# A four-layer modulated convolution: the third weight combination with 19 products in borrowed banks, and another order of the iterations from quad 4 on

## The chip, the core and the metric

The kernel runs on one core of one Trainium2 chip. The time is the device time of one execution in microseconds (us). Three executions of the kernel before gave 480.82, 481.82 and 482.02 us; their median, 481.82 us, is the time before.

## The reference

The input `x` holds 128 samples of 64 channels and 1024 positions, the style `cond_512` a vector of 128 for each sample. Four layers follow one another, and their result is added to `x`:

```python
TYPES = ('same', 'upsample', 'same', 'downsample')
s = style @ mw.T + mb
weight = SCALE * w * s[:, None, :, None]
demod = lax.rsqrt(jnp.sum(weight * weight, axis=(2, 3)) + EPS)
weight = weight * demod[:, :, None, None]
```

Each layer is a convolution with three taps of 64 by 64 channels, with the sample's own weights, and a bias. The second layer doubles the length and blurs, the fourth blurs and halves it. Nothing nonlinear lies between the layers, so for each sample the four of them are one convolution with nine taps, but for a few positions at both ends.

## The kernel before, in words

**The work.** Four samples make a *quad*; there are 32 quads, q = 0 to 31. The 128 partitions hold 64 channels of two samples, and two column blocks the other two, so each product appears as four matmuls of 64 rows by 64 columns (upper and lower half of the rows, upper and lower half of the columns). Everything is in 32-bit floats, and the profile shows each of these matmuls as two, eight for a product.

For each quad the nine taps are made first, in three *weight combinations* on TensorE (PE), each followed by ScalarE (ACT) copies that scale the result out of the PSUM accumulators:

- `stage1` combines the weights of layers 4 and 3 into the tile `S`. From quad 4 on it is split: `stage1_a` (three products, five blocks of 64 columns) and `stage1_b` (two products, two blocks). VectorE (DVE) forms two further blocks from the accumulators (L443), and GpSimd (POOL) adds one block into another (L446, called the S addition below).
- `stage2` applies the blur and layer 2 (tile `E`) and gives seven blocks `R`. In its plain form it has 9 products with 23 blocks (L533). Where it is *shared*, `share_sums` adds blocks of `S` on DVE (L462), `share` computes three products into unused columns of the accumulator `psA` of another quad (L467), `share_copy` lets ACT copy them into `psR` (L490), and `stage2_rest` adds the other 14 products. Quads 7 to 30 are shared.
- `stage3` (L574) combines `R` with layer 1 (`w0s`) to the nine taps `Wf`. It has 9 products: six in part 0 with 14 blocks and three in part 1 with 7 blocks, 21 blocks of 64 columns in all. ACT scales them into `Wf` (L361). 

**The convolution** of a quad is done in Winograd's way: positions come in threes, and five products `conv0` to `conv4` with 340 columns (each with three tap groups, 24 matmuls in the profile, all on L685) take the place of nine. Its inputs are sums of shifted rows of `x`: `in3`, `in_g01`, `in_g2` and `in04` on DVE, `in1` (L658) and `in2` (L663) on POOL from quad 4 on. `in1` and `in2` need the sums `G` that `in_g01` and `in_g2` leave. Its weights are sums of taps, `combine_a` and `combine_b` on DVE (tile `H`), and `residual` adds the identity. conv3 opens the accumulator `psA`, ACT copies it out (`copy_m3`), conv1 adds to it and DVE's `sum1` reads it; then conv2 adds to it, and DVE's `sum2` writes two results: the accumulator `Y` (the bank that conv4 adds to) and the tile `y`. conv0 adds to `psA` at the end. ACT scales the three results `psA`, `Y`, `y` into `o` (`output`, L753), and SP stores them. Loads of `x` are also on SP's queue.

**The order** is written out by hand: the loop at L1207 issues for each q the instructions of several quads, and each engine executes its own in that order. In iteration q the quad q ends (conv4, conv0, outputs), n = q+1 has conv3, conv1 and conv2, c = q+2 has stage2 and stage3 and its inputs, and s = q+4 (from q = 3 on) has stage1. The weight combinations use two PSUM banks, `ps_w`, one after another; `psA` has two buffers of two banks, `Y` two banks.

**One-time work** lies in the dictionary `EXTRA`, (q, place): the normalisations (`var_newton`), scale tables on POOL (`table_C` writes `tC`, the scale of `R`, for all quads from 8 on), and the outputs at both ends of the samples, which are computed apart: `SLOTS` names the iterations (9, 12, 14, 19) with an additional group of end products on PE in `Y`, and `setup_x`, `setup0`, `setup1`, `setup3`, `rest0` to `rest3`, `rest1_bias` and `blur_side` are their DVE steps. `ends3` in iteration 28 is the last end product, `rest3` and `rest3_bias` its DVE steps.

Of the kernel before, what the change touches and what calls it, by code (L numbers as in the profile page):

```python
# [55 lines left out]
K = 3  # L56
# [7 lines left out]
def kernel(  # L64
# [26 lines left out]
    r_pool = ctx.enter_context(tc.tile_pool(name="r_pool", bufs=4))  # L91
# [58 lines left out]
    Z = const.tile([P, 512], F32, name="Z")  # L150
# [272 lines left out]
    def stage1_a(q):  # L423

        ps = unit(ps_w, f"psS{q}")
# [25 lines left out]
    Ed = const.tile([P, 6, C], F32, name="Ed")  # L451
# [69 lines left out]
    def stage2(q, pool=None, engs=(nc_a, nc_a), between=None):  # L521
# [21 lines left out]
        rt = []  # L543
        for r in range(2):
            t = r_pool.tile([P, 7, C], F32, tag="R", name=f"R{q}_{r}")
            scaled_copy(
                engs[r], t.rearrange("c t o -> c (t o)"), ps[r][:, : 7 * C], tC[:, q, r : r + 1]
            )
            rt.append(t)
        chain[q] = rt  # L550
        return ps

    def stage3(q, part, pool=None, engs=(nc_a, nc_a)):

        rt = chain[q]
        ps = unit(pool or ps_w, f"psW{q}_{part}")
        if part == 0:
            Wq[q] = (
                wf_pool.tile([P, 2, K, K, C], F32, tag="Wf", name=f"Wf{q}"),
                wf_pool.tile([P, 3, 2, K, C], F32, tag="H", name=f"H{q}"),  # L560
            )
        W = Wq[q][0]
        kinds = ((0, 1), (2,))[part]
        n = 0
        for i, kind in enumerate(kinds):
            for k in range(K):
                gs = [g for g in range(K) if 0 <= K * g + kind - k < 7]
                lo, m = gs[0], len(gs)
                first = K * lo + kind - k
                n += 1  # L570
                for r, rows in enumerate(HALF):
                    for c, cols in enumerate(HALF):
                        at = (K * i + lo) * C
                        nc.tensor.matmul(  # L574
                            ps[r][cols, at : at + m * C],
                            w0s[kind][rows, k, :],
                            rt[c][rows, first : first + K * (m - 1) + 1 : K, :],
                            start=(n == 1),
                            stop=(n == K * len(kinds)),
                            skip_group_check=True,  # L580
                        )
        for r in range(2):
            dst = W[:, r, kinds[0] : kinds[-1] + 1].rearrange("c t g o -> c (t g o)")
            scaled_copy(engs[r], dst, ps[r][:, : len(kinds) * K * C], t0[:, q, r : r + 1])
        return ps

    def residual(q):

        W = Wq[q][0]
        for r in range(2):  # L590
            v = W[:, r, 1, 1, :]
# [5 lines left out]
    def taps(q):  # L597
        W, H_ = Wq[q]
        return *(W[:, :, i] for i in range(K)), *(H_[:, i] for i in range(3))
# [74 lines left out]
    def product(q, m, ps, groups=range(K)):  # L674
# [3 lines left out]
        for g in groups:  # L678
            for s, rows in enumerate(HALF):
                for c, cols in enumerate(HALF):  # L680
                    if m in (0, 4):
                        w = W[rows, c, m // 2, g, :]
                    else:
                        w = H_[rows, m - 1, c, g, :]
# [24 lines left out]

    def conv3(q, pool=None):  # L710
        A[q] = unit(pool, f"psA{q}") if pool else ps_conv.tile([P, 2, 512], F32, tag="u", name=f"psA{q}")
# [448 lines left out]
    def layers(i, j):  # L1160
# [4 lines left out]
        (1, 1): lambda: small_rest(1),  # L1165
# [26 lines left out]
        (28, 1): rest3,  # L1192
        (28, 2): rest3_bias,
# [5 lines left out]
    AHEAD = 3  # L1199

    def sharing(q):
        return AHEAD < q < NQ - 4
# [4 lines left out]
    for q in range(NQ):  # L1207
# [4 lines left out]
        if n == NQ:  # L1212
            for i, queue in enumerate((nc.sync, nc_a)):
                output(q, 1, i, nc_v)
                store(q, i, slice(1, 2), queue)
            conv4(q)
            for i, (eng, queue) in enumerate(zip(BOTH, (nc.sync, nc_a))):
                output(q, 2, i, eng)
                store(q, i, slice(2, K), queue)
            conv0(q, *range(K))  # L1220
            for i, (eng, queue) in enumerate(zip(BOTH, (nc_a, nc.sync))):
                output(q, 0, i, eng)
                store(q, i, slice(0, 1), queue)
            break
        if c < NQ:
            stage2(c)
        if n < NQ - 1:
            sum2(q)
        if n < NQ - 1:
            if q == 0:  # L1230
                in_g01(n)
            if q == 1:
                in_g2(n)
                load(n + NX)
            combine_a(n)
            combine_b(n)
            if q == 0:
                in_g2(n)
                load(n + NX)

        if n == NQ - 1:

            conv3(n)
            copy_m3(n)
            conv4(q, 0, 1)
            for i in range(2):
                output(q, 1, i)
            conv1(n)
            sum1(n)
            conv4(q, 2)  # L1250
            for i in range(2):
                output(q, 2, i)
                store(q, i, slice(1, K))
            in04(n, PAIR[0])
            in04(n, PAIR[1])
            conv0(q, 0)
            conv2(n)
            conv0(q, 1, 2)
            sum2(n)
            for i in range(2):  # L1260
                output(q, 0, i)
                store(q, i, slice(0, 1))
            continue

# [13 lines left out]
        if late(q):  # L1278
            for i in range(2):
                store(q, i, slice(2, K))  # L1280
            if late(q - 1):
                for i in range(3):
                    load(c + 1, slice(i, i + 1))
        if c < NQ:
            stage3(c, 0)
        conv3(n)
        copy_m3(n)
        if sharing(q) and not sharing(q - 1):
            share_sums(c + 1)
# [9 lines left out]
        if c < NQ:  # L1299
            stage3(c, 1)  # L1300
        if q in SLOTS:
            slot(*SLOTS[q], Y_banks)
        if s < NQ:
            conv0(q, 0)
# [7 lines left out]
        elif s < NQ:  # L1312
            stage1_a(s)
        elif q == NQ - 4:
            slot(ends3, 3, unit(ps_w, "psE"), 3)
        conv1(n, 1, 2)
        for i in range(2):
            output(q, 1, i)
            if late(q):
                store(q, i, slice(1, 2))  # L1320
# [6 lines left out]
        if n == NQ - 2:  # L1327
            combine_a(n + 1)
            combine_b(n + 1, (0,))
# [4 lines left out]
        conv0(q, *((1,) if s < NQ else (0, 1)))  # L1334
        if twice:
            stage1_a(s)
        elif s < NQ:
            stage1_b(s)
        if sharing(q + 1) and not twice:
            share_sums(s)  # L1340
        if sharing(q):
            share(c + 1, banks(q))
        conv0(q, 2)
        if sharing(q):
            share_copy(c + 1)
# [10 lines left out]
        if q and c < NQ - 1:  # L1356
# [3 lines left out]
        if s + 1 < NQ:  # L1360
            scale3(s + 1)
# [3 lines left out]
        if n == NQ - 2:  # L1365
            sum2(n, (0,))
            combine_b(n + 1, (1,))
            in1(n + 1, nc_v)
            sum2(n, (1,))
            combine_b(n + 1, (2,))  # L1370
            in2(n + 1, nc_v)
        for i in range(2):
            store(q, i, slice(0, 1 if late(q) else K))

# [77 lines left out]
```

## Time and profile before

| what | value |
|---|---|
| median of three executions | 481.82 us |
| the profiled execution, its own time | 482.28 us |
| its span, first to last instruction | 480.4 us |
| PE, busy | 98% of the span |
| DVE, busy | 83% |
| ACT, busy | 63% |
| POOL, busy | 29% |
| mean granted TensorE clock | 0.997 of full speed |

The span is what the views count from: a start of 203.24 us is 203.24 us after the first instruction. PE stands for TensorE's matmuls and PEld for its weight loads. In a group of instructions, "out<-in" names the tiles with their numbers left out, and "x24" how often the instruction is there. The chain of work that ended last is followed back from the last instruction, at each step to what released it. A matmul's own duration contains time in which others run beside it; where matmuls follow one another in the chain, the length of the piece is what they cost.

### The profile page before, as it was taken

Reading aid. Unit: us, or ns where it says so; the run is one execution under the profiler, and the core shown is the slowest. Engines: PE = TensorE matmul, PEld = TensorE weight load, DVE = VectorE, ACT = ScalarE, POOL = GpSimd, SP = SyncE. Lnnn points to the kernel's source line nnn. Section 1 sums busy time; section 2 is a strip of 40 time slices with the busy share of each in tenths; the row PEclk is TensorE's granted clock in tenths of the full one; section 3 lists DMA queues with packets and bytes.
Section 4 is the critical chain, followed back from the end, with each engine's and each line's share of the span. In section 5 each row is a group of like instructions: output and inputs, shape, how many; then the busy total and the mean of one; then the engine's idle time right before and its main releaser. Section 6 shows DMA issues by size and latency. Waiting matters only on the chain.

```text
span 480.4 us, 25778 instructions
## 1 busy us (share of the span) xinstructions
PE 472.2 (98%) x11592; PEld 369.2 (77%) x11592; DVE 399.0 (83%) x660; ACT 303.8 (63%) x620; POOL 138.9 (29%) x171
## 2 busy tenths in 40 slices
PE   8999999999999999999999999999999999999995
PEld 7977787888788777878777798767777887877762
DVE  4899998799898888878868898758988887777984
ACT  5466666666667666766666666667666666665442
POOL 2533032635413333302333212333112333322100
PEclk9999999999999999999999999999999999999998
DMA  7116364245555346544445545345544445554314
GB/s 243 53 63 194 118 195 191 92 149 172 164 159 149 115 138 180 163 136 140 141 137 178 150 150 145 125 148 161 165 142 129 151 150 180 169 157 151 106 60 175
DMA packets 50494, 70.65 MB, mean 147 GB/s; under 512 B 5648, under 2 KB 47312, under 8 KB 50384
## 3 DMA queue, kind: packets, MB, share of 16 engines
q1 hardware_dynamic: 49792, 68.32, 44.7%
q8 instruction: 91, 1.49, 1.3%
q10 hardware_dynamic: 592, 0.69, 0.4%
q14 instruction: 19, 0.16, 0.1%
HBM read 35.36 MB, written 33.62 MB: 144 GB/s over the span
## 4 chain that ended last, share of the span: by engine, by line
PE 97%; DVE 2%; issue 0%; ACT 0%; ACTq 0%; DVEq 0%
PE psA L685 45%; PE psW L574 15%; PE Y L685 11%; PE psR L467 10%; PE psS L390 6%; PE psR L533 4%; PE psA L467 2%; PE Y L921 2%; PE Y L337 1%; PE Y L181 1%; DVE Oe L1011 0%; PE psM L205 0%; DVE o L755 0%; DVE y L595 0%; PE psE L921 0%
## 5 line engine op out<-in xcount | busy, mean ns | idle before, releaser
L685 PE MATMUL psA<-T,H 64*64 64x340 f32 x2304 | 193.3, 446 | 1.2 <-DVE y L595 0.9
L685 PEld LDWEIGHTS psA<-T,H 64*64 64x64 f32 x2304 | 100.2, 133 | 46.6 <-issue 3.3
L446 POOL TENSOR_TENSOR S<-S 128x128 f32<-128x128 f32 x28 | 15.0, 536 | 268.7 <-ACT S L361 261.5
L595 DVE SCALAR_TENSOR_TENSOR G<-X 128x684 f32<-128x684 f32 (+1 forms) x65 | 76.2, 1207 | 0.0
L685 PE MATMUL psA<-T,Wf 64*64 64x340 f32 x768 | 74.8, 446 | 0.0
L361 ACT ACTIVATE R<-psR,tC 128x448 f32<-128x448 f32 x63 | 36.5, 630 | 43.4 <-PE psR L467 26.8
L361 ACT ACTIVATE Wf<-psW,t 128x384 f32<-128x384 f32 (+1 forms) x126 | 56.3, 497 | 11.1 <-PE psW L574 10.8
L685 PE MATMUL Y<-T,Wf 64*64 64x340 f32 x768 | 62.9, 447 | 0.2 <-issue 0.2
L574 PE MATMUL psW<-R,w0s 64*64 64x128 f32 (+1 forms) x1536 | 63.1, 287 | 0.0
L574 PEld LDWEIGHTS psW<-R,w0s 64*64 64x64 f32 x1536 | 53.2, 133 | 5.9
L595 DVE SCALAR_TENSOR_TENSOR Y<-m,psA 128x680 f32<-128x680 f32 x32 | 27.8, 870 | 33.3 <-PE psA L685 33.3
L663 POOL TENSOR_TENSOR T<-G 128x684 f32<-128x684 f32 x28 | 50.9, 1817 | 0.0
L467 PE MATMUL psR<-S,E 64*64 64x64 f32 (+1 forms) x1536 | 50.6, 237 | 0.2 <-issue 0.2
L672 DVE TENSOR_TENSOR T<-G 128x1368 f32<-128x1368 f32 (+1 forms) x33 | 50.6, 1536 | 0.0
L658 POOL TENSOR_TENSOR T<-G 128x684 f32<-128x684 f32 x28 | 46.5, 1660 | 13.1 <-DVE G L595 13.1
L753 ACT ACTIVATE o<-Y,tb,td 128x340 f32<-128x340 f32 x63 | 36.6, 630 | 19.3 <-PE Y L685 16.7
L467 PEld LDWEIGHTS psR<-S,E 64*64 64x64 f32 x1536 | 43.2, 134 | 5.1 <-issue 0.3
L595 DVE SCALAR_TENSOR_TENSOR y<-psA,m 128x680 f32<-128x680 f32 x32 | 27.7, 865 | 23.1 <-PE psA L685 20.6
L390 PEld LDWEIGHTS psS<-wd,w2n 64*64 64x64 f32 x1120 | 38.3, 133 | 9.5
L685 PEld LDWEIGHTS Y<-T,Wf 64*64 64x64 f32 x768 | 32.9, 133 | 13.9 <-issue 1.1
L753 ACT ACTIVATE o<-psA,tb,td 128x340 f32<-128x340 f32 x63 | 37.0, 644 | 8.0 <-PE psA L685 8.0
L361 ACT ACTIVATE S<-psS,tBn 128x256 f32<-128x256 f32 x56 | 23.5, 470 | 28.2 <-PE psS L390 28.2
(153 smaller groups left out, 703.6 us busy)
## 6 DMA issues: line engine op xcount, KB each, us to landing
out<-o SPq DMA_DIRECT2D x167, 170.0 KB, 2.7
X<-in_x SPq DMA_DIRECT2D x150, 172.0 KB, 3.5
X<-in_x SPq DMA_DIRECT2D x14, 516.0 KB, 4.9
out<-o SPq DMA_DIRECT2D x6, 510.0 KB, 5.6
out<-o SPq DMA_DIRECT2D x2, 340.0 KB, 2.7
Xe<-in_x_ends SPq DMA_DIRECT2D x1, 512.0 KB, 6.5
out<-o ACTq DMA_DIRECT2D x3, 170.0 KB, 3.1
par<-in_params SPq DMA_DIRECT2D x2, 192.0 KB, 3.3
```

What stands on the lines that cost most here:

```text
L361: nc_a.activation(dst, src, AF.Copy, scale=f)
L390: nc.tensor.matmul(ps[r][cols, at * C : (at + n) * C], weight[rows], wd[c if r == 0 else 1 - c][rows, taps], start=first, stop=last, skip_ ...
L446: nc_g.tensor_add(t[:, :, 2], t[:, :, 2], t[:, :, 0])
L467: nc.tensor.matmul(dst[r][cols], weight[rows], st[c if r == 0 else 1 - c][rows, slots, :], start=False, stop=last, skip_group_check=True,)
L533: nc.tensor.matmul(ps[r][cols, lo * C : (lo + m) * C], E[rows, e + 2, :], src[rows, a, :], start=(n == 0), stop=(n == 8), skip_group_check ...
L574: nc.tensor.matmul(ps[r][cols, at : at + m * C], w0s[kind][rows, k, :], rt[c][rows, first : first + K * (m - 1) + 1 : K, :], start=(n == 1 ...
L595: nc_v.scalar_tensor_tensor(out, x, f, y, op0=ALU.mult, op1=op)
L658: eng.tensor_add(t[:, :, 0, :NJ], plane(g, 2), plane(g, 1))
L663: eng.tensor_sub(t[:, :, 1, :NJ], plane(g, 2), plane(g, 1))
L672: nc_v.tensor_sub(t[:, pairs, :, :NJ], both(a, PL), both(b, 1))
L685: nc.tensor.matmul(ps[s][cols, :NB], w, Ts[q, tag][rows, c, i, g : g + NB], start=(g == 0 and m == 3), stop=(g == K - 1), skip_group_check ...
L753: nc_a.activation(dst, src, AF.Identity, bias=add, scale=d3)
```

## The change

1. `stage3` becomes two parts for quads 6 to 30. `stage3_b` opens the accumulator `psA` of quad n, before conv3 of quad n opens it anew, and computes seven products with 12 blocks. Two of its seven result blocks are shares: ACT copies them (times 1 and times 1/3, four copies of 128x128) into `ps_w`, and `stage3_a` adds four products with 7 blocks there. Together 19 blocks in 11 products, where there were 21 in 9. Three new operands come with it: `Wd` (two differences of weights, on POOL in iteration 1), and two further blocks of `R`, which DVE adds for each quad (`r_sums`, 128x256, both inputs in `R`).
2. `R` is one tile of 2x9 blocks with two buffers instead of one of 7 blocks for each half with four; `Wf` has its taps in the order of their making; `Z` is smaller, and `Ed` lies in a tile that is no longer needed.
3. The loop is split. Iterations 0 to 3 keep the order before (`early_turn`). Iterations 4 to 28 have a new one (`turn_of`, 4 with some exceptions as the *entry*), in which conv2 of a quad moves behind the next iteration's stage2. Iterations 29 to 31 are written out. The extras of an iteration, which stood at three places in it, all come at its end. Sharing begins at iteration 5, so quads 8 to 30 are shared. `rest3` takes the place of `in_g01` in iteration 28, and `rest3_bias` moves to iteration 29.

```diff
-    r_pool = ctx.enter_context(tc.tile_pool(name="r_pool", bufs=4))
+    r_pool = ctx.enter_context(tc.tile_pool(name="r_pool", bufs=2))
...
+    def r_sums(q):
+        t = chain[q]
+        nc_v.tensor_add(t[:, :, 7:9], t[:, :, 2:6:3], t[:, :, 3:7:3])
...
+    def stage3_b(q, ps):
+        new_w(q)
+        t = chain[q]
+        plan = (
+            (slice(0, 3), w0s[2][:, 2, :], slice(0, 7, 3)),
+            (slice(0, 2), w0s[2][:, 1, :], slice(1, 5, 3)),
+            (slice(0, 2), w0s[2][:, 0, :], slice(2, 6, 3)),
+            (slice(3, 4), w0s[0][:, 0, :], slice(0, 1)),
+            (slice(4, 5), w0s[1][:, 0, :], slice(1, 2)),
+            (slice(4, 5), w0s[1][:, 1, :], slice(0, 1)),
+            (slice(5, 7), w0s[0][:, 1, :], slice(7, 9)),
+        )
+        for i, (at, weight, slots) in enumerate(plan):
+            same_row(blocks(ps, at), weight, t, slots, i == 0, i == len(plan) - 1)
+        pw = shared_w[q] = unit(ps_w, f"psW{q}")
+        src = blocks(ps, slice(5, 7))
+        for i, f in enumerate((1.0, 1.0 / 3.0)):
+            for dst, v in zip(blocks(pw, slice(i, i + 3, 2)), src):
+                scaled_copy(nc_a, dst, v, f)
+        stage3_out(q, ps, 0, 5)
+
+    def stage3_a(q):
+        t, pw = chain[q], shared_w.pop(q)
+        plan = (
+            (slice(0, 3, 2), Wd[:, 0], slice(3, 7, 3)),
+            (slice(0, 3, 2), w0s[0][:, 2, :], slice(1, 5, 3)),
+            (slice(1, 4, 2), Wd[:, 1], slice(2, 6, 3)),
+            (slice(1, 2), w0s[1][:, 0, :], slice(4, 5)),
+        )
+        for i, (at, weight, slots) in enumerate(plan):
+            same_row(blocks(pw, at), weight, t, slots, last=i == len(plan) - 1)
+        stage3_out(q, pw, 5, 4)
...
-        (28, 1): rest3,
-        (28, 2): rest3_bias,
+        (29, 0): rest3_bias,
...
     def sharing(q):
-        return AHEAD < q < NQ - 4
+        return FIRST < q < NQ - 4
...
+    def turn_of(q):
+        n, c, s = q + 1, q + 2, q + 4
+        entry = q == FIRST
+        stage2(c)
+        r_sums(c)
+        if not entry:
+            conv2(q)
+        sum2(q)
+        if entry:
+            conv4(q)
+        stage3_b(c, open_a(n))
+        combine_a(n)
+        if entry:
+            conv0(q, 0, 1)
+        else:
+            conv4(q)
+        stage3_a(c)
+        combine_b(n)
+        conv3(n)
+        if entry:
+            copy_m3(n)
+        outputs(q, 2)
+        for i in range(3):
+            load(c + 1, slice(i, i + 1))
+        if s < NQ:
+            stage1_a(s)
+        else:
+            slot(ends3, 3, unit(ps_w, "psE"), 3)
+        if not entry:
+            copy_m3(n)
+        in04(n)
+        in3(c)
+        if q in SMALL:
+            l, bs = SMALL[q]
+            nc_v.memset(high(bs.stop - bs.start), 0.0)
+        in_g2(c)
+        conv0(q, *((2,) if entry else range(K)))
+        if entry:
+            conv1(n, 0, 1)
+        outputs(q, 1)
+        if s < NQ:
+            stage1_b(s)
+            in_g01(c)
+        else:
+            rest3()
+        if sharing(q):
+            share(c + 1, banks(q))
+            share_copy(c + 1)
+        outputs(q, 0)
+        if q in SLOTS:
+            slot(*SLOTS[q], Y_banks)
+        if q in SMALL:
+            small(q)
+        conv1(n, *((2,) if entry else range(K)))
+        sum1(n)
+        if s == NQ:
+            in_g01(c)
+        if sharing(q + 1):
+            share_sums(s)
+        in1(c, nc_g)
+        in2(c, nc_g)
+        for i in range(3):
+            extra(q, i)
+        if s + 1 < NQ:
+            scale3(s + 1)
+
+    for q in range(FIRST):
+        early_turn(q)
+    for q in range(FIRST, NQ - 3):
+        turn_of(q)
+
+    q, n, c = NQ - 3, NQ - 2, NQ - 1
+    stage2(c)
+    conv2(q)
+    stage3(c, 0)
+    sum2(q, (0,))
+    combine_a(n)
+    sum2(q, (1,))
+    conv4(q)
+    combine_b(n)
+    conv3(n)
+    outputs(q, 2)
+    copy_m3(n)
+    extra(q, 0)
+    in04(n)
+    in3(c)
+    in_g01(c)
+    stage3(c, 1)
+    conv0(q, 0)
+    conv1(n)
+    outputs(q, 1)
+    in_g2(c)
+    sum1(n)
+    combine_a(c)
+    combine_b(c, (0,))
+    conv0(q, 1, 2)
+    outputs(q, 0)
+    conv2(n)
...
```

More of the change, by code (lines that the diff above doesn't have):

```diff
@@ L1211 @@
             nc.sync.dma_start(Xe, x_ends)
[L1212 to L1263, printed above, removed]
+        stage2(c)
+        sum2(q)
+        if q == 0:
+            in_g01(n)
+        if q == 1:
+            in_g2(n)
+            load(n + NX)
+        combine_a(n)
+        combine_b(n)
+        if q == 0:
+            in_g2(n)
+            load(n + NX)
         conv4(q)
@@ L1355 @@
             load(c + NX)
-        if q and c < NQ - 1:
+        if q:
             in1(c, nc_g)
@@ new lines @@
+    conv0(q, 1, 2)
+    outputs(q, 0)
+    conv2(n)
+    sum2(n, (0,))
+    combine_b(c, (1,))
+    in1(c, nc_v)
+    sum2(n, (1,))
+    combine_b(c, (2,))
+    in2(c, nc_v)
+    q, n = NQ - 2, NQ - 1
+    conv3(n)
+    copy_m3(n)
+    conv4(q, 0, 1)
+    for i in range(2):
+        output(q, 1, i)
+    conv1(n)
+    sum1(n)
+    conv4(q, 2)
+    for i in range(2):
+        output(q, 2, i)
+        store(q, i, slice(1, K))
+    in04(n, PAIR[0])
+    in04(n, PAIR[1])
+    conv0(q, 0)
+    conv2(n)
```

178 lines of the change are left out of this document (100 added, 78 removed).

## The prediction

> **What bounds the kernel now.** I read the page first: busy times, then the engines' shares of the chain of work that ended last.
>
> ```profile
> span 480.4 us, 25778 instructions
> PE 472.2 (98%) x11592; PEld 369.2 (77%) x11592; DVE 399.0 (83%) x660; ACT 303.8 (63%) x620; POOL 138.9 (29%) x171
> PE 97%; DVE 2%; issue 0%; ACT 0%; ACTq 0%; DVEq 0%
> ```
>
> PE holds 97% of the chain, so PE work taken out is time gained, until something else ends last. What a turn (one iteration) costs, the chain in order of time tells; first the stage2 of a turn and of the next but one before it, then the pieces of one turn, then pieces from elsewhere.
>
> ```profile
> 189.30 1.94 PE psR L467 x90
> ...
> 203.24 1.94 PE psR L467 x91
> 205.17 1.72 PE Y L685 x24
> 206.89 1.52 PE psW L574 x48
> 208.41 1.72 PE psA L685 x24
> ...
> 430.61 0.35 PE psA L467 x24
> ...
> 440.57 0.76 PE psW L574 x24
> ...
> 88.83 2.50 PE psR L533 x72
> ```
>
> From one stage2 to the next are 203.24 - 189.30 = 13.94 us, and the pieces follow without a gap: five times 1.72 for the convolutions, 1.94 shared stage2, 1.52 + 0.76 stage3, the rest stage1 and share. Below, 0 is the end of a turn's stage2 (205.17 here), T4 the turn of iteration 4.
>
> **PE's saving.** 14 blocks took 1.52 us and 7 took 0.76: 0.109 a block. Three products of one block (share) took 0.35: 0.117 each. The new stage3 has 15 blocks in wide products and 4 single ones: 15 x 0.109 + 4 x 0.117 = 2.10 against 2.28, so 0.18 us a quad, 25 quads, **-4.5**. PE's turn is then 13.76. Quad 7 is no longer shared: 2.50 - 1.94 - 0.35 = **+0.2**.
>
> The new ACT copies (128x128, accumulator to accumulator) are not in the trace.
>
> ```profile
> L490 ACT COPY psR<-psA 128x256 f32<-128x256 f32 x48 | 15.2, 361 | 22.0 <-PE psA L685 21.0 <-DVE S L443 1.0
> L246 ACT ACTIVATE d<-psM,eps 128x16 f32<-128x16 f32 x1 | 0.3, 274 | 0.0
> ```
>
> Between these two rows, 0.27 to 0.36, I take 0.3. All four end 1.2 (at most 1.45) after stage3_b, beside conv4's 1.72: nothing on the path, 1.2 a turn if conv4 were not there. They stand before no output that anybody waits for sooner.
>
> **The DVE steps of the new order.** PE now meets conv4 at 1.72 (conv2) + 1.33 (stage3_b) = 3.05. It needs sum2's Y, and sum2 now stands on DVE behind r_sums, which waits for the ACT copies of R.
>
> ```profile
> 203.31 0.87 DVE L595 SCALAR_TENSOR_TENSOR Y<-m,psA 128x680 f32<-128x680 f32 x1 [1.35 <-PE psA L685]
> ...
> 205.27 1.16 ACT L361 ACTIVATE R<-psR,tC 128x448 f32<-128x448 f32 x2 [1.07 <-PE psR L467]
> ...
> 210.24 2.36 DVE L595 SCALAR_TENSOR_TENSOR G<-X 128x1376 f32<-128x1376 f32 x2
> ```
>
> R starts 0.10 after stage2 and ends at 1.26. sum2 must start by 3.05 - 0.87 - 0.05 = 2.13. Were r_sums free to run, it would take some 0.55 (0.43 to 0.83: share_sums below has the same form), and sum2 would start at 1.86: covered. But is it free? Its both inputs are in SBUF, and POOL's in1 and in2, which before ran in the middle of a turn, now come after in_g01, at the turn's end. What the two engines do to each other stands in the timelines of DVE and POOL, behind a row with the durations of share_sums (shortest, median, longest):
>
> ```profile
> L462 DVE TENSOR_TENSOR S<-S x24: 425/590/827, 94.0 to 417.4; 128x256 f32<-128x256 f32 x24
> ...
> 47.70 0.47 DVE L592 SCALAR_TENSOR_TENSOR Wf<-idn,t,Wf 128x64 f32<-128x64 f32 x2
> ...
> 58.39 0.86 DVE L595 SCALAR_TENSOR_TENSOR G<-X 128x684 f32<-128x684 f32 x1
> ...
> 59.40 1.66 POOL L658 TENSOR_TENSOR T<-G 128x684 f32<-128x684 f32 x1 [3.69 <-DVE G L595]
> 61.00 1.97 POOL L663 TENSOR_TENSOR T<-G 128x684 f32<-128x684 f32 x1
> ...
> 60.72 0.76 DVE L595 SCALAR_TENSOR_TENSOR H<-Wf 128x384 f32<-128x384 f32 x1
> 61.39 1.85 DVE L592 SCALAR_TENSOR_TENSOR Wf<-idn,t,Wf 128x64 f32<-128x64 f32 x2
> ...
> 199.60 0.46 POOL L446 TENSOR_TENSOR S<-S 128x128 f32<-128x128 f32 x1 [10.07 <-ACT S L361]
> 200.02 1.65 POOL L658 TENSOR_TENSOR T<-G 128x684 f32<-128x684 f32 x1
> 201.63 1.82 POOL L663 TENSOR_TENSOR T<-G 128x684 f32<-128x684 f32 x1
> 201.43 0.53 DVE L462 TENSOR_TENSOR S<-S 128x256 f32<-128x256 f32 x1
> ```
>
> Two DVE additions that take 0.47 undisturbed took 1.85 when in2 had begun: they ended 0.27 after in2 (62.97). H, ahead of them, had waited for in1's end (61.06), and in2 then waited for H (61.48). share_sums ended 0.29 after in1 (201.67), and in2 then 1.49 after share_sums. So a DVE operation with two SBUF inputs and a POOL operation take turns, whole instruction by whole instruction; sum2, which reads the accumulator, took its usual 0.87 beside in2. [...]
>
> From one sum2 to the next this makes a loop: 6.93 to the first G (210.24 - 203.31), 2.36 for in_g2 and in_g01, 0.55 for the two S operations that now lie between them, 0.25 for the S addition on POOL (0 to 0.46), 0.15 until POOL starts (59.40 against the end of the G before it, 59.25), in1 1.65, share_sums 0.29, in2 1.49, r_sums 0.21 until sum2 starts behind it: **13.9** (13.65 to 14.1). That is more than PE's 13.76, so in a plain turn DVE and POOL set the pace, and the 0.18 is nearly given back: 0.14 a turn.
>
> **Extras.** Each DVE extra stands between share_sums and r_sums, has two SBUF inputs, comes behind in2, and lengthens the loop by itself. In the order before they stood at mid-turn, with DVE idle for 1.35 ahead of sum2.
>
> ```profile
> L897 DVE TENSOR_TENSOR Xm<-Xe,sc 128x512 f32<-128x512 f32 x2 | 1.3, 684 | 0.0
> L937 DVE TENSOR_TENSOR Ye<-raw,a 128x384 f32<-128x384 f32 x2 | 1.1, 551 | 0.0
> L968 DVE SCALAR_TENSOR_TENSOR Ue<-b1s,Ue 128x576 f32<-128x576 f32 x2 | 1.5, 751 | 0.0
> L893 DVE SCALAR_TENSOR_TENSOR g<-par,g 128x192 f32<-128x192 f32 x4 | 1.4, 356 | 0.1
> L995 DVE TENSOR_TENSOR Ue<-Ve 128x576 f32<-128x576 f32 x2 | 1.4, 751 | 0.0
> ```
>
> Two at a time, less 0.1 for overlap: T8 1.2 (Xm), T10 and T11 1.05 each (Ye), T16 and T17 1.2 each (L968 and two of a third of it), T22 1.35 (L995). By width, estimates: T13 0.85, T15 0.75, T20 and T21 1.35, T23 1.2, T24 1.1, T6 0.7, T7 0.4. T9 has 1.4 (L893) and as much in eight small ones; its end product on PE covers all but 1.2. Sum 16.0. After a turn with an end product r_sums is on time, and 0.27 (2.13 less 1.86) of the next extra is hidden, three times: -0.8. With 0.14 for 15 plain shares: **+17.3**. These are the largest term; if in2 were out of the way, they would lie in the gap until R is ready, at no cost but T9's 0.7.
>
> **Once only.** *Entry, T4:* no conv2 covers stage2's end, and conv4 waits for R, r_sums and Y: 1.13 + 0.45 + 0.87 + 0.05 = 2.5 where sum2 before ran beside stage2. Later stage1_b waits for S copies queued behind copy_m3 and two outputs, and conv3 and stage2 a little: 0.95. **+3.45.** Its extra, a Newton step, and a late in2 delay T5's conv4 by **+1.5**. *T6:* R of quad 8 needs table_C, which POOL issues behind in2.
>
> ```profile
> 116.19 1.85 POOL L663 TENSOR_TENSOR T<-G 128x684 f32<-128x684 f32 x1
> 118.00 0.70 POOL L288 TENSOR_TENSOR tC<-dm 64x48 f32<-64x48 f32 x2
> ```
>
> Before, tC ended at 118.70, and stage2 at 119.30. Now it ends 3.9 after stage2 (in2 at 2.0, a Newton step in turns with it, tC), and R, r_sums and Y follow: 1.16 + 0.45 + 0.87, conv4 at 6.4 instead of 3.05: **+3.4**. *The end:*
>
> ```profile
> 433.26 1.93 PE psR L467 x111
> ...
> 442.23 1.41 PE psE L921 x22
> ...
> 444.01 2.37 DVE Oe L1011 x2
> ...
> 447.30 1.95 PE psA L685 x24
> 449.25 2.50 PE psR L533 x72
> ```
>
> ```profile
> L1023 DVE SCALAR_TENSOR_TENSOR Oe<-Oe,par_s,Xe 64x384 f32<-64x384 f32 x2 | 1.2, 608 | 0.0
> ```
>
> T28 lasted 449.25 - 433.26 = 15.99, and its pieces (1.94, five convolutions, 2.28, 1.41 for psE) come to 14.23: conv2 stood behind rest3 and sum1. The new order has a conv0 and a conv1 in that place: -1.8. In T29, however, DVE gets 1.2 of rest3_bias (L1023) and starts sum2 only after conv2, while conv2 of quad 30 needs sum1, last of that queue: sum2 at 1.8, then 6.93 + 2.36 + 1.23 of DVE work, sum1 from 12.3 to 13.2, against 10.9 on PE: 2.4, and 1.1 where H waits for in2. Together **+1.7**.
>
> Sum: -4.5 + 0.2 + 17.3 + 3.45 + 1.5 + 3.4 + 1.7 = +23.0. The profiled execution took 482.28 (1.9 beyond its span), 0.46 above the median; with the median, **504.8 us**.
>
> **Rivals.** (1) *DVE goes first or beside POOL at the turn's end.* For: share_sums did slip in between in1 and in2. Against: the 1.85 above, with in2 already waiting. Then extras cost 0.7, plain turns nothing, T5 nothing, T6 2.0, the end 0.6: -4.5 + 0.2 + 0.7 + 3.45 + 2.0 + 0.6 = +2.4, 484.3. (2) *POOL is through in time; not slower.* Place: the end of in_g01. If it came at about 10.3 instead of 12 after stage2, in2 would end before R is copied less the extra, table_C too, and DVE's queue would be ahead at the end: -4.5 + 0.2 + 3.45 + 0.6 or less = 481.5, below that if entry's waits overlap. Against: 9.8 of contiguous DVE rows after sum2's start. (3) *The products are fewer, but not shorter*: 44 matmul positions instead of 36. At 0.16 for each of the 4 single blocks the saving would be nothing: 509.3. Against: 0.117 in share.
>
> **How the numbers follow.** Forecast 0.63 (494 to 512), rival 1 0.14 (482.5 to 490), rival 2 0.13 (478 to 482.5), rival 3 0.06, anything longer 0.04. With 0.13 left out below and some 0.06 above, the range is 483 to 512; the loop's 13.65 to 14.1 alone is worth -5 to +4. A measurement here tells about 0.3% (1.4 us) from no change. Faster: most of rival 2, 0.09; the same: its rest and rival 1's low end, 0.06; slower 0.85.
>
> **What would show it.** In the chain after: plain turns near 13.9, those behind extras 14.7 to 15.4, T6 longest; Y's conv4 released by sum2, r_sums ending some 0.3 after in2. Wrong: turns of 13.76 with extras (rival 1), PE with no idle time after T6 (rival 2), stage3 parts of 2.28 together (rival 3). In the entry, conv4 should start 2.5 after stage2's end.

## The result, and the profile after

The changed kernel takes **513.07 us** (median of 6, 509.79 to 515.92) against 482.07 us of the kernel before on the same chip (6, 480.82 to 482.94): a ratio of 1.0643, with an interval of 1.0602 to 1.0684. The profiled execution took 514.02 us. Slower, as forecast, but by 31 us instead of 23, and 1 us above the range. Of all executions in this document one, of 504.61 us in experiment 6, was in a slower state of the chip, and without it that kernel's median is 497.01 us instead of 498.83. First the page: span, busy times, the granted clock in 40 slices.

```profile
span 512.2 us, 26699 instructions
PE 481.8 (94%) x11928; PEld 372.7 (73%) x11928; DVE 441.3 (86%) x684; ACT 313.3 (61%) x718; POOL 147.3 (29%) x173
PEclk9999999899899999999999999999999999999989
```

PE's share fell from 98% to 94%, though its combination is shorter, and the clock shows an 8 three times, twice early and once near the end. The chain of work that ended last now reaches back only to 484.56 us, so the turns are compared one by one, by the start of stage2's first matmul in both traces. T4 is the turn of iteration 4.

| stretch | before | after | difference | forecast |
|---|---|---|---|---|
| start to T3 | 88.57 | 88.78 | +0.2 | 0 |
| T4 | 14.50 | 17.46 | +3.0 | +3.3 |
| T5 | 14.08 | 16.04 | +2.0 | +1.5 |
| T6 | 14.10 | 18.09 | +4.0 | +3.2 |
| T7 to T27 | 301.82 | 319.55 | +17.7 | +13.5 |
| T28 | 15.98 | 14.10 | -1.9 | -2.0 |
| from T29's stage2 | 31.4 | 38.2 | +6.8 | +3.5 |
| span | 480.4 | 512.2 | +31.8 | +23.0 |

The forecast's terms are divided over the stretches here, with PE's 0.18 in each turn of T4 to T28. The view of waits, for PE: who waited, for whom; us in total, times, longest.

```profile
PE psA L572 <- issue: 7.5, 10, 1.7
PE Y L754 <- DVE Y L663: 5.3, 10, 2.5
PE psA L754 <- DVE y L663: 3.2, 2, 3.0
PE psA L572 <- DVE R L589: 2.3, 5, 0.7
PE psA L572 <- ACT R L361: 2.1, 1, 2.1
PE psR L468 <- issue: 1.6, 4, 0.7
```

The waits for Y and for R (L589 is r_sums) were forecast. 9.1 us of "issue", in which PE waited for nothing that the profile shows, were not; before, three such rows had 0.2 us each. What a forecast wait looks like, the timeline of T22 tells (stage2 starts at 369.48):

```profile
369.98 1.66 POOL L727 TENSOR_TENSOR T<-G 128x684 f32<-128x684 f32 x1 [2.13 <-DVE G L663]
...
370.59 1.33 DVE L463 TENSOR_TENSOR S<-S 128x256 f32<-128x256 f32 x1
...
371.60 1.83 POOL L732 TENSOR_TENSOR T<-G 128x684 f32<-128x684 f32 x1
371.69 1.16 ACT L361 ACTIVATE R<-psR,tC 128x448 f32<-128x448 f32 x2 [0.83 <-PE psR L468]
371.85 2.13 DVE L1013 TENSOR_TENSOR Ve<-raw,a 128x512 f32<-128x512 f32 x1
...
374.01 0.69 DVE L1014 TENSOR_TENSOR Ve<-Ve,c 128x512 f32<-128x512 f32 x1
...
374.62 0.42 DVE L589 TENSOR_TENSOR R<-R 128x256 f32<-128x256 f32 x1
374.95 0.86 DVE L663 SCALAR_TENSOR_TENSOR Y<-m,psA 128x680 f32<-128x680 f32 x1
...
375.87 1.95 PE L754 MATMUL Y<-T,Wf 64*64 64x340 f32 x24
```

share_sums (L463) ends 0.28 after in1 (371.64), the extra (L1013) takes 2.13 and ends 0.55 after in2 (373.43), r_sums starts 1.8 after R has been copied (372.85), and conv4 follows Y: it starts 6.39 after stage2's start, where 4.99 (1.94 + 3.05) would be without a wait. This is the loop of the forecast.

### The profile page after: what moved, and what is told of

Same layout as the page of the kernel before. It is cut to its first block, busy times and chain, and to the rows that moved or that the text cites. A ratio compares the mean times of both kernels' runs of the same rounds, so it can differ in the third digit from the quotient of the medians.

```text
span 512.2 us, 26699 instructions
## 1 busy us (share of the span) xinstructions
PE 481.8 (94%) x11928; PEld 372.7 (73%) x11928; DVE 441.3 (86%) x684; ACT 313.3 (61%) x718; POOL 147.3 (29%) x173
## 5 line engine op out<-in xcount | busy, mean ns | idle before, releaser
L754 PE MATMUL psA<-T,H 64*64 64x340 f32 x2304 | 190.2, 449 | 3.4 <-DVE y L663 3.2
L446 POOL TENSOR_TENSOR S<-S 128x128 f32<-128x128 f32 x28 | 23.4, 835 | 230.3 <-ACT S L361 230.3
L663 DVE SCALAR_TENSOR_TENSOR G<-X 128x1376 f32<-128x1376 f32 (+2 forms) x65 | 78.8, 1215 | 0.2 <-DMA X<-in_x 0.2
L754 PE MATMUL psA<-T,Wf 64*64 64x340 f32 x768 | 64.5, 446 | 0.0
L361 ACT ACTIVATE psW<-psA 128x128 f32<-128x128 f32 x100 | 19.3, 268 | 70.0 <-PE psA L572 60.5
L361 ACT ACTIVATE Wf<-psW,t 128x256 f32<-128x256 f32 (+2 forms) x76 | 32.7, 480 | 30.6 <-PE psW L572 30.3
L468 PE MATMUL psR<-S,E 64*64 64x64 f32 (+1 forms) x1472 | 48.4, 237 | 1.3 <-issue 1.3
L572 PEld LDWEIGHTS psA<-R,w0s 64*64 64x64 f32 x1000 | 36.4, 137 | 14.8 <-issue 8.3
L572 PE MATMUL psA<-R,w0s 64*64 64x64 f32 (+2 forms) x1000 | 38.4, 268 | 8.5 <-issue 6.4
L754 PEld LDWEIGHTS psA<-T,Wf 64*64 64x64 f32 x768 | 32.5, 133 | 12.2
```

Source lines behind the costliest of these rows:

```text
L361: nc_a.activation(dst, src, AF.Copy, scale=f)
L446: nc_g.tensor_add(t[:, :, 2], t[:, :, 2], t[:, :, 0])
L468: nc.tensor.matmul(dst[r][cols], weight[rows], st[c if r == 0 else 1 - c][rows, slots, :], start=False, stop=last, skip_group_check=True,)
L572: nc.tensor.matmul(dst[r][cols], weight[rows], t[rows, c, slots, :], start=first, stop=last, skip_group_check=True,)
L663: nc_v.scalar_tensor_tensor(out, x, f, y, op0=ALU.mult, op1=op)
L754: nc.tensor.matmul(ps[s][cols, :NB], w, Ts[q, tag][rows, c, i, g : g + NB], start=(g == 0 and m == 3), stop=(g == K - 1), skip_group_check ...
```

## What could explain the rest

- **A, DVE and POOL:** extras and r_sums wait out in2, as forecast. Rival: DVE just has too much to do.
- **C, the clock:** a long stop of PE is followed by a stretch at half clock. Rival: the low clock has another cause.
- **F, instruction fetch:** the "issue" stops are PE out of instructions, because a fetch lands late. Rival: a wait that the profile does not name; or the stops lie beside the waits for Y and cost nothing.
- Rival to all three: the new products cost what they should save.

## The experiments

Every ratio is against the kernel before on the same chip.

**1. The order alone.** The 21 products back in the new order:

```diff
-        r_sums(c)
...
-        stage3_b(c, open_a(n))
+        stage3(c, 0)
...
-        stage3_a(c)
+        stage3(c, 1)
```

> The new order alone, with the old 21 products and without r_sums and fills. Theory A: PE gets 0.18 us a quad more work, but r_sums (0.42 us of the DVE-POOL loop) goes, so turns that DVE sets gain 0.4 and turns that PE sets lose 0.18; the stop in the entry, the one in the sixth turn and the one at the end stay, with the granted clock of 0.5 behind each: 508 to 516 us. Rival (the products cause the loss): 485 to 490 us.

506.95 us (1.0508, 1.0483 to 1.0533). That is 1 us below what I expected and far above the rival's 485 to 490. The order costs 25 us, the new products in this order 6 more: not what they should save, but not the loss either. The 6 are no price of a plain turn: of the 8.7 us between the two traces 5.7 lie in T4 to T6, where only the changed kernel has stretches at half clock (experiment 4), and 3.0 in T7 to T27.

**2. The products alone**, in an order that I wrote for them: stage2, conv4 (two groups), stage3_b, the rest of conv4 and a group of conv0, stage3_a, conv0, conv3, stage1_a, conv1, stage1_b, share, conv0, conv2.

> The new third combination alone, in an iteration that keeps the old order's cover: stage2 is followed by two thirds of conv4, conv2 stays at the turn's end, in1 and in2 run in mid-turn on POOL, sum2 stands first on DVE and r_sums behind combine_a. Theory A (the new order lost the time, the products gave their 0.18 us a quad): plain turns of 13.76 to 13.8 us against 13.94, turns with an extra up to 0.5 more since DVE's and POOL's operations that exclude each other now fill the turn; 476 to 481 us, no granted clock of 0.5 in mid-run, no long stop of PE behind the instruction fetches. Rival (the new products cost more than they save, by the wait for r_sums and the four fills): 484 us or more, with PE waiting for R or psW in every turn.

515.48 us (1.0702, 1.0670 to 1.0735) instead of 476 to 481: the expectation fell. T23 lasted 16.16 us, with three stops of PE (from start to start of two matmuls): 1.23 without a wait in stage2, 0.54 ahead of conv1, which needs copy_m3, and 0.43 ahead of conv2, which needs sum1. By their place I had made the covers of the last two too short; the trace names no releaser for them. So the run says nothing on the products, but that stops without a wait come with another order too.

**3. The extras.** T8 to T24's DVE extras left out (first), and in2 moved to where DVE reads an accumulator (second; its tile has one buffer, so it waits for conv2):

```diff
             conv2(q)
+            in2(n, nc_g)
         sum2(q)
...
         in1(c, nc_g)
-        in2(c, nc_g)
```

> The changed kernel without the DVE extras of the turns 8 to 24, whose results it leaves out: the tiles of the ends stay zero. Theory A (each extra behind in2 delays r_sums, sum2 and conv4 of the next turn): the turns 9 to 25 fall from 14.6 to 15.4 us to 13.76 to 14.0, except where PE stops without a wait (issue): 496 to 501 us, the waits of conv4 for Y nearly gone outside of the entry and the sixth turn. Rival B (the stops without a wait set these turns, the waits for Y only lie beside them): 508 us or more.

> The changed kernel with in2 moved on POOL from the turn's end to behind conv2 of the next turn (its tile has one buffer, so that it waits for conv2), where DVE's sum2 and the subtraction behind it read the accumulator and run beside it. Theory A (extras and r_sums wait out in2): the loop of DVE and POOL loses 1.49 of 13.9 us, share_sums stays behind in1, an extra then runs in the gap until R is ready, r_sums starts within 0.05 us of R's end in nearly every turn, turns 9 to 25 are 13.75 to 14.0 us but for stops without a wait: 501 to 504 us, as without the extras (502.1). Rival (DVE has too much to do with an extra, wherever in2 runs): 508 us or more.

502.07 us (1.0408, 1.0366 to 1.0449) and 504.52 us (1.0469, 1.0436 to 1.0502): -11.0 and -8.6. Theory A holds and its rival falls: with all its extras and the same DVE work, only in2 elsewhere, the kernel gains most of what leaving the extras out gains. Both times are 0.5 to 1 us above what I expected, and PE's rows on issue were still at 5.7 and 9.6 us.

**4. The once-only stops.** sum2 ahead of r_sums in the entry, table_C and the Newton steps ahead of in1 and in2, sum1 ahead of in_g01 in T29, the ends' bias later:

```diff
+        if entry:
+            sum2(q)
+            r_sums(c)
...
+        if q < 6:
+            extra(q, 0)
         in04(n)
```

> The changed kernel with its three once-only stops taken away by moved operations: in the entry sum2 ahead of r_sums, in the fourth and fifth turn the Newton steps and table_C ahead of in04 and so ahead of in1 and in2, at the end sum1 ahead of in_g01 and in_g2 and the bias of the ends later. Theory with the clock (a stop of 2.5 us or more is followed by 3.4 us at half clock, 1.7 us more): all three stretches at 0.5 go, 2.96 + 1.97 + 3.99 us of the fourth to sixth turn and 3 to 5 at the end: 499 to 503 us. Rival (only the stops themselves cost, the clock was granted low for another reason): stretches at 0.5 stay somewhere, 503 to 507 us.

504.09 us (1.0460, 1.0437 to 1.0483), -9.0, 1 us less than expected: T4 to T6 44.2 instead of 51.6 us, T28 to the end 50.4 instead of 52.3, less than I expected there, since the stop moved to conv3, which then waited 1.8 for H. The trace has no stretch at half clock in mid-run (PEclk is 9 in all 40 slices). That the stop and half clock are two prices, this kernel doesn't show, but a pair does: the changed kernel and one of experiment 5 (phase). Windows of 3.41 us in the changed kernel's entry: busy time of PE, PEld, DVE, ACT and POOL, PEclk (1.00 is full speed), DMA share, GB/s.

```profile
90.78:94.19 3.41, 0.95 (x26) 0.60 (x22) 1.48 (x3) 1.16 (x2) 3.11 (x9) 1.00 0.02 5
94.19:97.60 3.41, 3.41 (x28) 1.60 (x28) 3.31 (x8) 0.00 (x0) 0.12 (x1) 0.50 0.00 0
```

The same in a kernel of experiment 5, where conv4's wait is the same but begins elsewhere in the windows:

```profile
90.14:93.55 3.41, 2.42 (x71) 2.06 (x62) 0.00 (x0) 1.23 (x3) 3.10 (x7) 1.00 0.23 71
93.55:96.96 3.41, 1.96 (x32) 1.15 (x36) 3.20 (x7) 0.14 (x1) 1.76 (x4) 1.00 0.00 0
```

The timelines of PE, the changed kernel first, then that of experiment 5:

```profile
94.01 3.55 PE L754 MATMUL Y<-T,Wf 64*64 64x340 f32 x24 [2.46 <-DVE Y L663]
```

```profile
95.00 1.95 PE L754 MATMUL Y<-T,Wf 64*64 64x340 f32 x24 [2.45 <-DVE Y L663]
```

With the same wait of 2.46 or 2.45 us T4 takes 17.46 us or 15.75: half clock is worth 1.71 there. Two more stops stand in kernels with and without half clock behind them. T6, where PE waits 2.1 for R, takes 18.09 us in the changed kernel and 16.76 in experiment 3's first (no_extras); from the end of T29's wait of 3.0 to PE's last matmul it is 15.58 us in the changed kernel, and 14.24 in no_extras and in both kernels of experiment 5. That is 1.33 and 1.34. The records of the changed kernel's clock have the half three times while PE works, for 3.413 us each, from 94.19, 128.33 and 490.14, which lie 10 and 106 times 3.413 apart: a grid. In these traces, from 20 us on, a window of it in which PE ran no matmul for 2.06 us or more (in2_late, experiment 3) was followed by half clock, and one with 1.97 or less (old_products, experiment 1; a shorter wait, or one across a boundary) was not. So the window was not idle as a whole: 2.06 of 3.41 us without a matmul were enough.

**5. The fetch.** The stop in T26 of the changed kernel, from PE's timeline:

```profile
433.65 0.94 PE L572 MATMUL psA<-R,w0s 64*64 64x192 f32 x24
434.41 0.29 PE L572 MATMUL psA<-R,par 64*64 64x64 f32 x8
435.85 0.46 PE L572 MATMUL psA<-R,w0s 64*64 64x64 f32 x16 [1.14 <-issue]
```

R had been copied at 433.37, and r_sums was done at 434.21. And the two queues that move most, of which the second carries instructions (packets, MB, share of 16 engines):

```profile
q1 hardware_dynamic: 49792, 68.32, 42.4%
q8 instruction: 94, 1.54, 1.3%
```

94 packets of 16 KB for PE's 24,008 instructions (11928 matmuls, as many weight loads, and 152 others) make one packet for 256. So I counted PE's instructions in order of start up to each stop:

```
kernel     resumes at   stop   PE instructions   above 256 x n   last packet landed
changed      160.49     0.96        7105              193           1.45 before
changed      207.85     2.00        9409              193           1.44 before
changed      325.58     0.90       15553              193           1.29 before
changed      435.85     1.36       21185              193           1.44 before
phase        402.16     1.59       19649              193           1.54 before
phase        461.93     2.13       22721              193           1.39 before
old_order    361.75     1.69       17345              193           1.44 before
```

(Stops are from start to start of two matmuls.) In the changed kernel 14 stops of over 0.4 us in stage2 and stage3_b were without a wait; all 14 stand at 193. So do two of the three stops of 0.2 us in the kernel before. Two runs test it, one that shifts the count, one that relieves the queues:

```diff
+    zeros_to_y(16, 8, False)
```

> The changed kernel with 32 tiny products of zeros (128 more PE instructions) in its first 3 us, nothing else. In the changed kernel every stop of PE without a wait in stage2 and stage3 stands where the count of PE's instructions is 193 beyond a multiple of 256, the size of one instruction fetch. Theory F (PE runs out of fetched instructions): each such stop stands at 193 beyond a multiple of 256 again, so at code 128 instructions earlier; the 2.0 us in the turn of quad 13 and the 1.36 and 1.06 us in the last full turns go, others come, some 3 us more in all: 513 to 519 us. Rival (a wait that the profile does not name): the stops stay at the same lines of the same turns, 513 us and the cost of 64 tiny matmuls, at most 2 us.

```diff
+            queue.dma_start(out[q, :, s, at : at + 16], os[q][:, s, planes.start, :16])
```

> The changed kernel with the stores of quads 4 to 28 cut to 16 of 340 columns; the rest of the output is left unwritten. Theory F with the DMA engines as cause (a fetch stands behind the bursts of stores and loads): from the 129th instruction of a block to the start of its fetch a median of 2.5 us falls to 2.0 or less, stops without a wait fall from 9 us of PE idle to under 4, and 3 to 6 us of time go: 507 to 510 us. Rival (the fetch is as late whatever the queues do; only the dense run of instructions matters): 512 to 514 us and the same stops.

513.22 us (1.0659, 1.0616 to 1.0702) and 509.11 us (1.0550, 1.0518 to 1.0582). In the first the stops moved to other lines and other turns, as the table has it, and again to 193: they hang on the count of instructions and not on a wait of that place. The sum stayed instead of growing by 3: half clock was gone from T4 and from the end, and stops from T11, T19 and T27, while T22 and T28 got new ones (T28 lasted 16.17 us instead of 14.10). In the second, -4.0. The time from a block's 129th instruction to the start of the packet behind it (that origin is my choice, good for comparisons only) has a median of 2.0 us in the kernel before, 2.5 in the changed one, 2.2 here. So both parts matter, how late a fetch is and where in the code it is needed.

**6. Together, and with fewer bytes.** The mends and the late in2 in one kernel; that with nearly no traffic (16 columns of each store and load, so nearly all of the data is left out); that with the loads spread over the turn.

```diff
+            if planes.stop - planes.start == 1:
+                at = slice(at.start, at.start + 16)
```

> The three mends of once-only stops and the late in2 together. Theory A: the two gains add up, 9.0 and 10 to 12 us: 492 to 495 us; what is left above the 482.2 of before are the stops without a wait, the fifth turn and the end. Rival: the stops without a wait take the place of the waits for Y, and less than half of the second gain is left: 498 us or more.

> The kernel with the mends and the late in2, and with nearly no traffic beside the instruction fetches from quad 4 on: stores of quads 4 to 28 and loads of quads 7 on cut to 16 columns of each plane (most of the output unwritten, most of the input old). Theory F: with the DMA engines free a fetch starts 1.1 to 1.5 us after it is due instead of 2.7, the 12.6 us of PE idle without a wait in stage2 and stage3 fall under 2, and the time goes from 498.8 to 486 to 489 us. Rival (the fetch needs its time whatever else runs): over 495 us.

> The kernel with the mends and the late in2; the three planes' loads of a turn, which stood in one row behind the stores of the third output, stand one behind each output's stores. Theory F: the same bytes in smaller bursts, so a fetch is late less often; 2 to 6 us of the 12.6 us of stops go: 493 to 497 us. Rival (the mean load of the DMA engines counts, not the burst): 498 to 500 us.

497.01 us (1.0336, 1.0292 to 1.0381), 484.49 (1.0042, 1.0029 to 1.0055) and 496.44 (1.0267, 1.0222 to 1.0311). The gains of 9.0 and 8.6 made 16.1 together, and the kernel is still 2 us above the 492 to 495 expected. Without traffic it is 12.5 us faster: in the second the median delay is 1.5 us, no stop from T4 on stands at 193, and T15 to T18, T20 and T22 to T25 last 13.75 us each, with extras ahead of most. Spreading the loads gave 0.6 us, which the two intervals do not tell from nothing; 9.6 us on issue stayed in stage3_b.

**7. The traffic at another time.** All bytes again, but the stores of two outputs and the loads stand behind a transfer of one number of the next turn's R, in the stretch where I took no fetch to be urgent: ahead of T26's stop in the changed kernel the block's 129th instruction started at 430.12, the packet at 433.25, and R was copied at 433.37. Then the same edit alone in the changed kernel (after_gate).

```diff
+    def release(c):
+        nc.sync.dma_start(mark[:1, :1], chain[c][:1, 0, 0, :1])
+        for at in held:
+            store(*at)
...
         stage2(c)
+        release(c)
+        for i in range(3):
+            load(c + 1, slice(i, i + 1))
```

> The kernel with the mends and the late in2; the stores of a turn's second and first output and the loads stand in SP's queue behind a transfer of one number of the next turn's R, so that they run in the stretch from R's copy to conv3, and only the third output's stores lie elsewhere. The fetch that is needed in stage2 and the first part of stage3 falls due at the end of the turn before, when the DMA engines are then idle. Theory F: the stops without a wait fall from 12.6 us to under 4, 498.8 becomes 486 to 490 us with all the bytes moved. Rival (with the full traffic some fetch is always late): over 494 us.

> The changed kernel with the gate for stores and loads alone, so with the extras behind in2 and the once-only stops. If the late fetches cost the changed kernel itself some 4 to 6 us of the 31, as the cut stores suggest: 506 to 509 us, the stops without a wait under 3 us. Rival (there they lie beside the waits for Y and cost nothing): 511 to 514 us.

486.57 us (1.0095, 1.0057 to 1.0133): 10.4 us gained by the time of the transfers alone. In the changed kernel 508.50 (1.0545, 1.0526 to 1.0564), -4.6: that is the fetches' price there. The rest of their 9.1 us lay where PE would have waited anyway: its waits for Y and for r_sums' R rose from 7.6 to 13.7 us. With the stops gone, the longest waits are forecast ones:

```profile
PE Y L754 <- DVE Y L663: 7.1, 15, 2.5
PE psA L572 <- DVE R L589: 6.6, 12, 0.7
PE psA L754 <- DVE y L663: 3.2, 2, 3.0
```

**8. The last five us.** Small moves in the gated kernel: the ends' zeroing from T7 to T1, T9's extras spread (all three versions); H of quad 30 ahead of sum2 (first); conv2 of quad 29 back ahead of stage2, covered by the ends' product (second); one Newton step to T6 and the ends' rest to DVE's gap in T29 (third).

> As the one with the gate, and four small moves: the zeroing of a piece of Y ahead of the Newton steps in the fifth turn, the zeroing of the ends' tiles from the seventh turn to the first, the extras of the ninth turn spread over the turns 7, 9 and 18, and the H of quad 30 ahead of sum2 in turn 29. From the traces 1.0 us in the fifth, 0.9 in the seventh, 1.4 in the ninth and tenth and 1.5 to 2.2 us in the last turns: 4 to 5 us less than with the gate alone, 481 to 486 us; by the theory at its best under the 482.3 of before.

> The gated kernel with other small moves: one Newton step of the fifth turn behind the zeroing of Y's piece; the ends' zeroing in the first turn and the extras of the ninth spread; at the end conv2 of quad 29 back in front of stage2 with the ends' product as cover for sum1, the rest of the ends in the last turn but one. From the traces 0.85 in the fifth turn, 1.0 in the seventh and eighth, 1.9 in the ninth and tenth (the earlier fix showed these 1.9) and 2 to 2.6 us at the end: 480 to 482 us, by then PE's saving shows: 0.2 to 0.5 % under the 482 of before. Rival (something else is late there, as it was with the earlier fix): 484 us or more.

> The kernel before this one with two moves: the Newton step and table_3 from the fifth turn's end to the sixth's, and the rest of the ends from the last turn but one, where Y waited 1.2 us for it, to the gap of DVE ahead of sum1 in turn 29. From the trace 1.1 to 1.3 us in the sixth turn and 1.2 to 1.5 at the end: 478.8 to 480 us, 0.4 to 0.6 % under the kernel before, the first version in which PE's saving of 0.18 us a quad shows in the sum. Rival (the once-only waits only move on): 481.5 us or more.

489.30 us (1.0154, 1.0132 to 1.0176), a miss: T9 and T10 gave 2.2 us back, but H of quad 30 was caught behind in1 and in2. Its timelines of DVE and POOL in T29:

```profile
451.57 3.26 DVE L660 SCALAR_TENSOR_TENSOR Wf<-idn,t,Wf 128x64 f32<-128x64 f32 x2
...
451.26 1.89 POOL L728 TENSOR_TENSOR T<-G 128x684 f32<-128x684 f32 x1 [11.13 <-DVE G L663]
453.12 1.63 POOL L733 TENSOR_TENSOR T<-G 128x684 f32<-128x684 f32 x1
```

Two additions that take 0.47 together elsewhere took 3.26, until 0.1 after in2's end, Y came late, PE stopped 3.5, and half clock followed: conv4's 24 matmuls took 3.47, the next 24 1.89. The second version: 481.65 us (0.9998, 0.9987 to 1.0009). The third: **480.29 us (0.9965, 0.9954 to 0.9976), faster than the kernel before and than the changed one.** The 0.35% are clear of the interval, but small: 1.6 us of the 4.5 that PE saves, since T7 (15.84 us instead of 14.09) and the stretch from T29's stage2 (32.6 instead of 31.4) take 2.9 back. Its timeline of T23 (stage2 from 360.53), against that of T22 above:

```profile
360.94 1.66 POOL L728 TENSOR_TENSOR T<-G 128x684 f32<-128x684 f32 x1 [2.08 <-DVE G L663]
...
361.64 1.25 DVE L463 TENSOR_TENSOR S<-S 128x256 f32<-128x256 f32 x1
...
362.73 1.16 ACT L361 ACTIVATE R<-psR,tC 128x448 f32<-128x448 f32 x2 [0.82 <-ACT wd L361]
362.80 1.42 DVE L1072 TENSOR_TENSOR Ue<-Ve 128x576 f32<-128x576 f32 x2
363.39 0.59 SPq L1297 DMA_DIRECT2D mark<-R  x1
364.03 1.87 SPq L835 DMA_DIRECT2D out<-o  x4
364.14 0.41 DVE L589 TENSOR_TENSOR R<-R 128x256 f32<-128x256 f32 x1
...
364.48 0.86 DVE L663 SCALAR_TENSOR_TENSOR Y<-m,psA 128x680 f32<-128x680 f32 x1
364.54 1.65 POOL L733 TENSOR_TENSOR T<-G 128x684 f32<-128x684 f32 x1 [1.94 <-PE psA L755]
...
365.51 1.89 PE L755 MATMUL Y<-T,Wf 64*64 64x340 f32 x24
```

The extra (L1072) runs undisturbed and ends 0.3 after R has been copied (363.89), Y runs beside in2, both at their usual length, and conv4 starts 4.98 after stage2's start, with no wait. Seven turns from T21 to T27 last 13.75 each. Its waits of PE, but for the start:

```profile
PE psA L755 <- ACT Wf L361: 1.1, 1, 1.1
PE psA L755 <- DVE y L663: 0.4, 2, 0.2
PE Y L755 <- DVE Y L663: 0.2, 1, 0.2
```

The first is in T7 (15.84 us), where a once-only wait has moved to; it wasn't taken away.

## Why the prediction was wrong, point by point

**What bounds it** held: where nothing is late, a turn is PE's.

**PE's saving**, 0.18 us a quad and a turn of 13.76: 13.75 against 13.94 measured. Rival 3 (shorter in number only) is out. But the same step counts blocks, not instructions: 44 matmul positions instead of 36 are 32 PE instructions more a turn, and they have to be fetched.

**The loop of DVE and POOL**, 13.9 us and each extra on top: right. With fetches on time (after_gate) T26 and T27, which have no extra ahead of them, last 13.88 and 13.90. T9 to T25 last 258.7 us there and 241.9 in the best version: the extras and the loop cost 16.8, forecast some 16 for these turns. Lone plain turns behind a turn with an end product went at PE's 13.75, as sum2 had been on time there. The rule that I drew from rows, that an operation of DVE with two inputs in SBUF and one of POOL take turns (0.47 us became 1.85), carried all of it, and rival 1 is out. Rival 2, POOL through in time, is what moving in2 made true.

**Once only.** The entry's 2.5 us wait for Y was 2.46; the turn, however, cost 1.25 without half clock (15.75 in the phase run against 14.50) and 3.0 with it, forecast 3.3: the 0.95 for later waits was not there, and 1.0 more was won in the turn that I have not followed. T5: 2.0 for 1.5. T6: 4.0 for 3.2, 1.3 of it half clock; R was late behind table_C as forecast, but PE stood at stage3_b, which reads R, and not at conv4. T28: -1.9 for -2.0. The end: 6.8 for 3.5, 1.3 of it half clock, 0.6 a longer wait for sum1's y (3.0 for 2.4), the rest in pieces that I have not followed.

**The step that failed** is the sum itself: "Sum: -4.5 + 0.2 + 17.3 + 3.45 + 1.5 + 3.4 + 1.7 = +23.0". It takes PE's pieces at their durations wherever PE is not waiting for data. Two terms are missing. The first is late instruction fetches, 4.6 us by the medians (after_gate). By the traces T7 to T27 last 319.55 us, and 314.5 with fetches on time, which is 12.7 above the kernel before where 13.5 were forecast; so the forecast is 4.2 short there. The second is three stretches at half clock, 1.71, 1.33 and 1.34, together 4.4 us. An entry and a T6 that I had sized 2.0 and 0.5 too long hid part of it, and T5 and the end's other waits, 0.5 and 2.0, added to it: 23.0 + 4.2 + 4.4 - 2.5 + 2.5 makes 31.6 of the 31.8. That the time came out only 1 us above the range owes something to these errors against each other. The trace before showed little of either: three stops of 0.2 us on issue, and half clock only behind PE's last matmul. Half clock came from an order in which PE stood still (2.46, 2.1 and 3.0 us), the late fetches from when the stores and loads run, as experiment 7 showed; and the range went up to 512 only for the sizes of known terms.

What stays open: why a fetch starts up to some 5 us after the 129th instruction when the queues are full (1.0 at the least, with traffic and without). That it does so was shown by taking the traffic away and by moving it, not how.

## What to carry to other kernels

Before an order by hand is changed, ask not only which engine waits for which, but what runs beside what: here operations on DVE and on POOL cost each other nothing where the one on DVE read an accumulator (Y 0.86 us, in2 1.65, experiment 8), and took turns where both its inputs were in SBUF (0.47 us became 1.85 and 3.26). In this unrolled kernel the program itself was a stream that had to arrive, 24,008 PE instructions in 94 packets of 16 KB: count instructions per us, and keep bursts of loads and stores away from the stretch ahead of the densest code (10.4 us in experiment 7). And three stops of PE, of 2.1 to 3.0 us, cost 1.33 to 1.71 us each on top here: remove the few long ones first, since whether they do depends on where they fall.

## What the runs showed of the hardware that I had not expected

- PE stopped at one count of instructions modulo 256 (193) when a packet of 16 KB of instructions landed late, up to 2.1 us at a time (phase), and went on 1.2 to 1.6 us after it had landed. Nothing marked it in the trace but "issue". 10.4 us of 497 hung on the time of the stores and loads alone.
- Half clock came for one window of 3.413 us on a fixed grid, if PE had been idle for some 2 us or more of the window before (2.06 was enough, 1.97 was not): 2.46 us of waiting brought it in one kernel, 2.45 did not in another, and 3.7 across two windows (in2_late) did not.
